# Gated scan layer with a mixture of experts: C's row to its bank by ScalarE, three places for its products, first loads in parts, the norm in pairs, the logits turned inside a product

## Chip, cores and metric

The kernel runs on one core of a Trainium2 chip. The metric is the device time of one execution in microseconds (us). The core's engines are named as in the profile: PE (TensorE), PEld (its weight loads), DVE (VectorE), ACT (ScalarE), POOL (GpSimd) and SP (SyncE, which here only issues DMAs). Each engine runs its own instructions in program order; where this text says that something is queued behind something else, it is this order that is meant.

## What is computed

The input `x` is 4 batches of 512 rows by 512, all float32. Two residual steps are made:

```python
x = x + tanh(g_xattn) * ssm(ctx, z=layernorm(x))      # for each of the 4 batches
x = x + tanh(g_ffn)   * moe(layernorm(x))

# ssm: 512 channels e, 512 times l, 16 states n
u     = silu(conv4(in_proj(ctx)) + b)                 # 512 x 512
dt_lo, B, C = split(x_proj(u))                        # 16, 16 and 16 rows
delta = softplus(dt_proj(dt_lo) + bias)
state[e,n] = state[e,n] * exp(delta[e] * A[e,n]) + delta[e]*u[e]*B[n]   # over l
y[e]  = sum_n state[e,n] * C[n] + D[e]*u[e];  y *= silu(z)

# moe: one shared expert for every row, and for every row the 3 best of 7 experts
p   = softmax(x @ gate_w + gate_b); best 3 of p + biases; weights p / sum of the 3
out = ffn(x, shared) + sum over the 3 of w * ffn(x, expert)
ffn(x, w1, wg, w2) = (silu(x @ w1) * (x @ wg)) @ w2
```

## The kernel before

**Layout.** Channels lie on the partitions, in 4 blocks of 128 (`c`), and times along the free axis. A *step* of a scan loop takes one state `k` and two channel blocks (`W = 2`), so a batch has 32 steps. A step is: POOL multiplies the B row by `delta*u` into `h` (`product`, L581, 128x1024), ACT makes two decays `da = exp(delta*A)` in PSUM (`decay`, L592), DVE runs two scans (L615), and then `finish` (L530 and on) multiplies `h` by the C row and adds the result up.

**Front (L411).** The first batch's projection, convolution, `x_proj` and softplus are made alone. They begin with `in_w` (L93) and the first context `cT` (L103), each one DMA of 512 KB on SP's queue.

**First loop (`loop(0)`, batch 0).** Nothing of the experts runs yet, so TensorE adds up: the products `hc = h*C` are added into four PSUM banks `sums` by an identity (L548). From step 4 on the rule of L525 to L530 holds: every third step's product (`n % 3 == 2`) is made by POOL, which reads the C row from `bc` (the B and C rows, spread over the partitions by DMA, two states to a load of 1 MB), and the other two by DVE, which reads the C row from a PSUM bank, `c_bank`. TensorE writes that bank once for every state:

```python
            if sums is not None and n >= per_load - 1 and c0 + W == NC and k + 1 < NS:
                row = DR + NS + k + 1
                nc.tensor.matmul(
                    c_bank, ident[0:NX, row : row + 1].to_broadcast([NX, P]), ly.xd, start=True, stop=True
                )
```

DVE's `hc` alternate between two places by `n % 2`; POOL's have one of their own. The first loop also carries `ahead_delta`, the projections and half of the softplus of batch 1, one piece to a step (`todo`), and `early`, one piece to every second step: the shared expert's three weights of 1 MB, the clearing of two DRAM tables by `xs<-empty` in 6 DMAs of up to 6 blocks (L177), and the load of batch 1's `x`.

**After a loop (`post(q)`, L677).** For the batch just scanned `y` is turned (L690), added to `x` with statistics (`add_y`, L692), normalised (`row_scale`, L207: a small DVE operation and a power on POOL; `norm`, L698), turned again (`turn_xn`) and copied by ACT (`copy_xn`, L709). All four blocks of 128 rows wait for one `row_scale`.

**Experts (`experts(q)`, L986).** A generator with 54 places to stop, here called pieces 0 to 53. Its head is piece 0 to 12: gate logits `pl` and `lg`, four small turns of the logits `pg` (L762), then the products of the shared expert `p1s` and `p2s` by quarters (`half`, L1005) with silu (`sgs`) and gating (`hidden`) between them, the routing on DVE cut into pieces (`route`, L749), the scatter of rows to `xs` by POOL (L869), and the shared output `pos`. Then 13 tiles of 128 gathered rows follow, three pieces each: a product with `w1`, one with `wg`, one with `w2`, two turns of blocks, and a scatter-add of rows to the output (`add_rows`).

**The order between the two.** The loops of batches 1 to 3 run inside the experts of batches 0 to 2. How many scan steps are issued after which piece is written out by hand in the table `STEPS`: for each `q` one string for `post` and one for `experts`, a digit for each piece. In these loops DVE makes every product with C and every addition (L530, L541). The preparation of batch `b + 2` (`ahead`, L359) is advanced by one piece in pieces 9 to 51 (`prepare`, L1045).

Of the kernel before, what the change touches and what calls it, by code (L numbers as in the profile page):

```python
# [10 lines left out]
F32 = mybir.dt.float32  # L11
# [6 lines left out]
P = 128  # L18
NS = 16
DR = 16  # L20
# [14 lines left out]
    0: ("000000", "010111110011010010101102100111110010011101111101101001"),  # L35
    1: ("100000", "111000110012000200010120111110110110001110111101100101"),
    2: ("001000", "021011010010111100101110200201011100102110010000000000"),
    3: ("000000", "000000000000000000000000000000000000000000000000000000"),
}
# [3 lines left out]
def gated_ssm_moe(  # L43
# [49 lines left out]
    nc.sync.dma_start(in_w, in_wT.rearrange("(k p) e -> p k e", p=P))  # L93
# [4 lines left out]
    def load_ctx(b):  # L98
        if b == 1:
            cT = homes[4][:, 0:NK, :]  # L100
        else:
            cT = one.tile([P, NK, L], F32, tag="cT", name=f"cT_{b}")
        nc.sync.dma_start(cT, ctxT[b].rearrange("(k p) l -> p k l", p=P))  # L103
        return cT
# [68 lines left out]
    def clear():  # L173

        nc.sync.dma_start(acc[(B - 1) * L : (B - 1) * L + P, :], empty[0][:, 0:D])
        for dst, src in zip(xs, empty):
            for i in range(0, NSLOT, 6):  # L177
                k = min(6, NSLOT - i)
                nc.sync.dma_start(
                    dst[i * P : (i + k) * P, :].rearrange("(i p) d -> p i d", p=P),  # L180
                    src.unsqueeze(1).to_broadcast([P, k, D + NW]),
                )
                yield
# [23 lines left out]
    def row_scale(mv, what):  # L207

        n = mv.shape[1]
        ve = small.tile([P, n], F32, tag="ve", name=f"ve_{what}")  # L210
        nc.vector.tensor_scalar(ve, mv[:, :, 1], EPS, None, ALU.add)
        rstd = small.tile([P, n], F32, tag=f"rstd{what[0]}", name=f"rstd_{what}")
        nc.gpsimd.tensor_tensor(rstd, ve, mhalf[:, 0:n], ALU.pow)
        return rstd
# [144 lines left out]
    def ahead(ly):  # L359


        for c in range(NC):
            ly.in_proj(c)
            yield 0.0
            ly.last_tap(c)
            yield 0.0
            ly.other_taps(c)
            later.append(lambda c=c: ly.silu(c))
            yield 2.3

        for _ in range(3):
            if later:
                yield 0.0
        flush()
        ly.x_proj()
        yield 0.0
        ly.rows_out()
        yield 0.0
        for c in range(NC):
            ly.dt_proj(c)  # L380
            yield 0.0
            ly.abs_relu(c)
            if c + 1 < NC:
                yield 0.0
        for c in range(NC):
            ly.exp(c)
        yield 0.0
        for c0 in range(0, NC, 2):
            for c in range(c0, c0 + 2):
                ly.log(c, own=True)  # L390
            yield 0.0
            for c in range(c0, c0 + 2):
                ly.soft(c)
                yield 2.5

    def ahead_delta(ly):
        ly.x_proj()
        yield 0.0
        ly.rows_out()
        ly.dt_proj(0)  # L400
        yield 0.0
        for c in range(NC):
            ly.abs_relu(c)
            if c + 1 < NC:
                ly.dt_proj(c + 1)
                yield 0.0
        for c in range(NC):
            ly.exp(c)
        yield 0.0
# [71 lines left out]
    def loop(b, sums):  # L481
# [29 lines left out]
        def finish(n, h):  # L511
# [3 lines left out]
            cost = 0.0  # L515
            if sums is not None and n >= per_load:
                next(todo, 0.0)
                if n % 2 == 0:
                    next(early, None)
            hc = h if sums is None else held[-1][:, n % 2]  # L520
            late = False
            c_k, engine = ly.bcs[k // NG][:, 1, k % NG, :], nc.vector
            if sums is not None and n >= per_load:

                if n % 3 == 2 and n < last:  # L525
                    engine, late = nc.gpsimd, True
                    hc = one.tile([P, W, L], F32, tag="cT", name=f"hc_{n}")
                else:
                    c_k = c_bank
            engine.tensor_tensor(hc, h, c_k.unsqueeze(1).to_broadcast([P, W, L]), ALU.mult)  # L530
            if sums is not None and n >= per_load - 1 and c0 + W == NC and k + 1 < NS:
                row = DR + NS + k + 1
                nc.tensor.matmul(
                    c_bank, ident[0:NX, row : row + 1].to_broadcast([NX, P]), ly.xd, start=True, stop=True
                )
            if sums is None:
                if nxt is not None and n >= last - W and nxt.n_mul < nxt.n_du:
                    nxt.mul(nxt.n_mul)
                    cost += 0.7
# [18 lines left out]
            return cost  # L558

        def ready(layer, n):  # L560

            k, c0 = steps[n]
            cost = 0.0
            for c in range(c0, c0 + W):
                if k == 0 and layer.n_soft == c:
                    layer.soft(c)
                    cost += 1.4
                if k == 0 and layer.n_mul == c:
                    layer.mul(c)
                    cost += 0.7  # L570
            return cost
# [26 lines left out]
        for n, (k, c0) in enumerate(steps):  # L598
            i = n % per_load
            cost = 3.6 if sums is not None else 4.8  # L600
            if h_before is not None:
                cost += finish(n - 1, h_before)
            if n not in ly.hs:
                cost += ready(ly, n)
                product(ly, n)
            if n not in ly.das:
                decay(ly, n)
            if n < last:
                cost += ready(ly, n + 1)
# [28 lines left out]
            if n >= last - 1 and sums is None:  # L638
                flush()
                gate(n - last + 1)  # L640
                cost += 0.7
            h_before = h
            if n == len(steps) - per_load - 1:

                for d in preps.pop(b + 1, ()):
                    cost += d
            if n == 2 and b > 0 and nxt is not None:
                ctxs[b + 1] = load_ctx(b + 1)
            if b > 0 and k // NG == 5:
                norm_x(b, i)  # L650
                cost += 0.9
            if b > 0 and k // NG == 6 and i == 1:
                szs = silus_x(b)
            yield cost
# [5 lines left out]
        cost = finish(last, h_before)  # L660
# [5 lines left out]
        for d in todo:  # L666
            cost += d
        yield cost + (2.0 if sums is not None else 2.7)
# [8 lines left out]
    def post(q):  # L677
# [20 lines left out]
        def norm(t):  # L698
            nc.vector.tensor_scalar(
                xns[:, t, 0:D], xx[:, t0 + t, :], mv[:, t, 0:1], rstd[:, t : t + 1],  # L700
                ALU.subtract, ALU.mult,
            )
# [14 lines left out]

        each(turn_y, pairs[0])
        yield 1.6, 0.0
        for k, pair in enumerate(pairs):  # L720
            each(add_y, pair)
            if k + 1 < len(pairs):
                each(turn_y, pairs[k + 1])
                yield 1.6, 3.2
        rstd = row_scale(mv, f"f_{q}")
# [5 lines left out]
        yield 0.0, 3.4, True  # L731
        each(norm, pairs[0])
        yield 0.0, 1.4
        for k, pair in enumerate(pairs):
            if k > 0:
                each(copy_xn, pairs[k - 1])
            else:
                for more in pairs[1:]:
                    each(norm, more)
            each(turn_xn, pair)  # L740
            yield 1.8, (1.4 if k == 0 else 0.0)
# [242 lines left out]
    SLOT = 3.75  # L984

    def experts(q):  # L986
# [6 lines left out]
        part = SLOT * nt / NC  # L993
# [11 lines left out]
        def half(k, hc):  # L1005
            pool, tag = (((ps_h, "p1"), (ps_o, "po")), ((ps_h, "p2"), (ps_t, "pt")))[k][hc % 2]
            (p1s, p2s)[k][hc] = mm(
                pool, tag, f"p{k + 1}s_{q}_{hc}", lambda c: ws.t[k][:, c, ts(hc, P)], lambda c: xnT[:, c, :], M
# [11 lines left out]
        yield part, 0.0, True  # L1020
        for hc in range(NC):
            if hc > 0:
                sgs(hc - 1)
            next(way, None)
            if adds:
                adds.pop(0)()
            half(0, hc)
            if hc == 1:
                next(way)
            yield part, (2.8 if hc == 1 else 0.0), hc > 0  # L1030
# [9 lines left out]
            yield part, (0.4, 4.8, 0.7, 0.7)[hc], hc < 2 or None  # L1040
# [3 lines left out]

        def prepare():  # L1045

            return next(preps.get(b + 2, iter(())), 0.0)
# [22 lines left out]
        yield SLOT, prepare(), True  # L1070
        hidden(NC - 1)
        W[1].load(1)
        second(1, range(1, NC - 1))
        second(2, range(2))
        yield SLOT, 0.7 + prepare()
        for i in range(4):
            xt[i] = rows_in(q, i)
        for t in range(2):
            second(t, [NC - 1])
        second(2, range(2, NC))  # L1080
        yield SLOT, prepare()
# [3 lines left out]
        yield SLOT, 0.75 + prepare()  # L1085
# [27 lines left out]
        for i in range(last_tile + 1):  # L1113
# [25 lines left out]
            yield SLOT, 0.7 + prepare()  # L1139
# [12 lines left out]
            yield SLOT + 0.6, prepare()  # L1152
# [25 lines left out]
            yield SLOT + 0.6, prepare(), True  # L1178
# [11 lines left out]
        yield SLOT + 0.6, 0.7, False  # L1190
# [3 lines left out]
        yield SLOT, 0.0  # L1194
# [10 lines left out]
    def moe():  # L1205
# [4 lines left out]
        at = {(q, k): count() for q in range(len(CHUNKS)) for k in range(2)}  # L1210
        for q, (b, _, _) in enumerate(CHUNKS):
# [3 lines left out]
            for _ in posts[q]:  # L1215
                yield q, 0, next(at[q, 0])
            banks = SOME
            for _ in experts(q):
                yield q, 1, next(at[q, 1])
                if q + 1 < len(CHUNKS) and CHUNKS[q + 1][0] in loop_done:  # L1220
                    others, banks = banks, SOME[:2]
                    piece = next(posts[q + 1], None)
                    banks = others
                    if piece is not None:
                        yield q + 1, 0, next(at[q + 1, 0])
# [77 lines left out]
```

## Time and profile before

| | us |
|---|---|
| median of 3 runs | 1098.37 |
| lowest and highest of them | 1097.23 and 1102.14 |
| the profiled execution: its own time | 1101.86 |
| the profiled execution: its span in the profile | 1099.7 |

The profile is of one execution. Its lines give, for groups of instructions, the line of the kernel, the engine, the operation, the tile written and the tiles read, how often, the time busy, the mean time of one in ns, and the idle time before them with what ended it. In the trace a time is counted from the start of the span. The stages, by their main lines: the front until 39 us, the first loop until 168, the first `post` until 194, the experts of batch 0 until about 440, of batch 1 until about 677, of batch 2 until about 894, and those of batch 3, with no loop beside them, until the end.

| engine | busy us | share of the span |
|---|---|---|
| PE | 971.8 | 88% |
| DVE | 795.9 | 72% |
| ACT | 537.7 | 49% |
| POOL | 495.7 | 45% |

### The profile page before, as it was taken

The page shows a single profiled execution, that of the slowest core. Times are in us where ns is not written, and L with a number is a line of the kernel's source. Part 1 is how long each engine was busy: PE and PEld are TensorE (multiplying, and loading weights), DVE is VectorE, ACT ScalarE, POOL GpSimd, SP SyncE. Part 2 cuts the span into 40 slices and gives each one's busy share as a digit, 9 for nine tenths or more (in the row PEclk, how much of TensorE's full clock was granted, in tenths as well). Part 3 has the DMA queues.
Part 4 walks back from the last instruction along what each step waited for, and adds up shares of the span by engine and source line. Part 5 has one row for each costly group of instructions (what it writes and reads, how often), then busy time and mean ns, then how long its engine had stood idle before and what let it go on. Part 6 is the DMA issues. An engine that isn't in the chain of part 4 may idle for free. (4 is left out here: it accounts for less than half of the span.)

```text
span 1099.7 us, 8888 instructions
## 1 busy us (share of the span) xinstructions
PE 971.8 (88%) x2532; PEld 432.4 (39%) x2532; DVE 795.9 (72%) x988; ACT 537.7 (49%) x747; POOL 495.7 (45%) x322
## 2 busy tenths in 40 slices
PE   7479885869999987979999889879999989999995
PEld 2123232324444434434444444334444534444442
DVE  5879887899999999879999998889988321100000
ACT  4566342365588674436597745536574220112211
POOL 1277980392463655572555545754554115011111
PEclk9579788989999999999999999989999999999998
DMA  3136920097999876589899936788999657999974
GB/s 123 58 133 208 362 91 27 10 356 229 336 325 343 292 258 221 143 310 333 303 329 317 355 105 212 258 278 319 308 367 316 194 174 255 344 314 331 322 243 96
DMA packets 137914, 272.10 MB, mean 247 GB/s; under 512 B 17006, under 2 KB 17006, under 8 KB 137854
## 3 DMA queue, kind: packets, MB, share of 16 engines
q1 hardware_dynamic: 126334, 244.71, 64.0%
q0 software_dynamic: 11328, 26.42, 10.4%
q8 instruction: 26, 0.43, 0.1%
q10 hardware_dynamic: 192, 0.26, 0.1%
q14 instruction: 34, 0.28, 0.1%
HBM read 230.65 MB, written 40.71 MB: 247 GB/s over the span
## 5 line engine op out<-in xcount | busy, mean ns | idle before, releaser
L581 POOL TENSOR_TENSOR h<-bc,home 128x1024 f32<-128x1024 f32 x128 | 309.6, 2425 | 248.1 <-DVE home L541 194.2
L917 PE MATMUL p<-w,turned_x 128*128 128x512 f32 x832 | 383.0, 605 | 22.5 <-ACT h L1157 16.5
L615 DVE TENSOR_TENSOR_SCAN h<-da,h 128x512 f32<-128x512 f32 x256 | 297.5, 1207 | 18.6 <-POOL h L581 10.1
L592 ACT ACTIVATE da<-home,a_neg 128x512 f32<-128x512 f32 x256 | 174.2, 689 | 248.1 <-DVE h L615 246.4
L917 PEld LDWEIGHTS p<-w,turned_x 128*128 128x128 f32 x832 | 155.4, 193 | 206.4 <-issue 172.5
L917 PE MATMUL po<-w,turned_h 128*128 128x512 f32 x416 | 189.9, 600 | 10.8 <-ACT yo L951 7.3
L956 POOL DMA_INDIRECT out_dram<-yo,row x52 | 97.3, 1871 | 220.1 <-ACT yo L951 188.4
L1096 DVE TENSOR_TENSOR h<-h,p 128x512 f32<-128x512 f32 x52 | 35.1, 675 | 156.5 <-PE p L917 151.8
L530 DVE TENSOR_TENSOR h<-h,bc 128x1024 f32<-128x1024 f32 x96 | 129.7, 1351 | 1.1
L541 DVE TENSOR_TENSOR home<-home,h 128x1024 f32<-128x1024 f32 x96 | 117.5, 1224 | 3.1
L917 PEld LDWEIGHTS po<-w,turned_h 128*128 128x128 f32 x416 | 75.6, 191 | 90.1 <-issue 76.2
L548 PE MATMUL sum<-hc,ident 128*128 128x512 f32 x128 | 75.3, 737 | 21.2 <-DVE hc L530 20.0
L869 POOL DMA_INDIRECT xs<-xn,place x48 | 55.1, 1147 | 41.9 <-issue 25.1
L1055 PE MATMUL pos<-w_s,home 128*128 128x512 f32 x128 | 60.6, 623 | 10.6 <-DVE home L1016 5.6
L917 PE MATMUL p1s<-home,w_s 128*128 128x512 f32 x128 | 62.0, 629 | 8.5 <-ACT sgs L1013 8.5
L909 ACT COPY turned_x<-pt_x 128x512 f32<-128x512 f32 x52 | 30.2, 580 | 79.0 <-PE pt_x L904 79.0
L592 ACT ACT_TABLE_LOAD x50 | 64.2, 1283 | 0.9
L951 ACT ACTIVATE yo<-po,weight 128x512 f32<-128x512 f32 x52 | 35.4, 681 | 53.6 <-PE po L917 46.1
L917 PE MATMUL p2s<-home,w_s 128*128 128x512 f32 x128 | 57.9, 595 | 0.0
L909 ACT COPY turned_h<-pt_h 128x512 f32<-128x512 f32 x52 | 30.1, 580 | 52.5 <-PE pt_h L904 52.4
L548 PEld LDWEIGHTS sum<-hc,ident 128*128 128x128 f32 x128 | 27.4, 226 | 67.1 <-issue 33.2
L1157 ACT ACT_TABLE_LOAD x36 | 46.2, 1283 | 0.5
(142 smaller groups left out, 828.5 us busy)
## 6 DMA issues: line engine op xcount, KB each, us to landing
w<-in_w_dram SPq DMA_DIRECT2D x104, 1024.0 KB, 8.2
w<-in_wg_dram SPq DMA_DIRECT2D x52, 1024.0 KB, 8.8
bc<-rows SPq DMA_DIRECT2D x32, 1024.0 KB, 5.9
xt<-xs SPq DMA_DIRECT2D x52, 256.0 KB, 5.9
xs<-empty SPq DMA_DIRECT2D x6, 1560.0 KB, 10.3
w_s<-in_ws_dram SPq DMA_DIRECT2D x8, 1024.0 KB, 9.9
xx<-in_x_dram SPq DMA_DIRECT2D x4, 1024.0 KB, 7.6
w_s<-in_wsg_dram SPq DMA_DIRECT2D x4, 1024.0 KB, 11.7
```

The lines of the kernel that those rows point to most:

```text
L530: engine.tensor_tensor(hc, h, c_k.unsqueeze(1).to_broadcast([P, W, L]), ALU.mult)
L541: nc.vector.tensor_tensor(y[:, c0 : c0 + W, :], y[:, c0 : c0 + W, :], h, ALU.add)
L548: nc.tensor.matmul(sums[c1 + w], ident, hc1[:, w, :], start=False, stop=(k1 == NS - 1))
L581: nc.gpsimd.tensor_tensor(h, b_k.unsqueeze(1).to_broadcast([P, W, L]), layer.u[:, c0 : c0 + W, :], ALU.mult)
L592: nc.scalar.activation(da, layer.delta[:, c, :], AF.Exp, scale=a_neg[:, c, k : k + 1])
L615: nc.vector.tensor_tensor_scan(h[:, w, :], da, h[:, w, :], 0.0, ALU.mult, ALU.add)
L869: put = nc.gpsimd.indirect_dma_start(xs[q % 2], bass.IndirectOffsetOnAxis(ap=place[:, t, k : k + 1], axis=0), xns[:, t, :], None)
L909: nc.scalar.copy(t, pt)
L917: nc.tensor.matmul(p[:, 0:n], lhs(c), rhs(c), start=(c == 0), stop=(c == NC - 1))
L956: nc.gpsimd.indirect_dma_start(acc, bass.IndirectOffsetOnAxis(ap=slot_of[q][1][:, i : i + 1], axis=0), yo, None, compute_op=ALU.add,)
L1055: nc.tensor.matmul(pos[t], hTs[:, c, ts(t, P)], ws.t[2][:, c, :], start=(c == 0), stop=(c == NC - 1))
L1157: nc.scalar.activation(hs[i], p1.pop(i), AF.Silu)
```

## The change

Each part in a sentence. (1) `c_bank` is written by a ScalarE copy from `bc` and no more by TensorE. (2) The products with C have three places, by `n % 3`, in all of the first loop. (3) `in_w` comes in two DMAs on SP's queue and the first context in two DMAs on ACT's queue. (4) `early` advances at every step and clears in 12 DMAs of up to 3 blocks. (5) `ahead_delta` has more places to stop, and its four exponentials stand in four pieces. (6) In `post`, `row_scale` is made for each pair of blocks. (7) In the head of the experts the turns of the logits stand in the middle of the first quarter product, after its second block. (8) The load `W[1].load(1)` is issued after the four `rows_in`. (9) The digits of `STEPS` are others. (10) The costs that the generators yielded are gone, and `prepare` is replaced by a table `PIECES` with ones at pieces 9 to 51 for batches 0 and 1, as before.

```diff
 STEPS = {
-    0: ("000000", "010111110011010010101102100111110010011101111101101001"),
-    1: ("100000", "111000110012000200010120111110110110001110111101100101"),
-    2: ("001000", "021011010010111100101110200201011100102110010000000000"),
+    0: ("000000", "011011000210010100110201110111110100110101101201101001"),
+    1: ("100000", "201000110010110110110101210110110110001101201101110001"),
+    2: ("000001", "021011010010102100110110110200200102002011010000000000"),
...
-    nc.sync.dma_start(in_w, in_wT.rearrange("(k p) e -> p k e", p=P))
+    for k in range(NK):
+        nc.sync.dma_start(in_w[:, k, :], in_wT[ts(k, P), :])
...
+        if b == 0:
+            for k in range(NK):
+                nc.scalar.dma_start(cT[:, k, :], ctxT[b, ts(k, P), :])
...
-            for i in range(0, NSLOT, 6):
-                k = min(6, NSLOT - i)
+            for i in range(0, NSLOT, 3):
+                k = min(3, NSLOT - i)
...
     def ahead_delta(ly):
         ly.x_proj()
-        yield 0.0
+        yield
+        yield
         ly.rows_out()
+        yield
         ly.dt_proj(0)
...
         for c in range(NC):
             ly.exp(c)
-        yield 0.0
+            yield
...
             if sums is not None and n >= per_load:
-                next(todo, 0.0)
-                if n % 2 == 0:
-                    next(early, None)
-            hc = h if sums is None else held[-1][:, n % 2]
+                next(todo, None)
+                next(early, None)
+            hc = h if sums is None else (held[-1][:, n % 3] if n % 3 < 2 else one.tile([P, W, L], F32, tag="cT", name=f"hc_{n}"))
...
             if sums is not None and n >= per_load - 1 and c0 + W == NC and k + 1 < NS:
-                row = DR + NS + k + 1
-                nc.tensor.matmul(
-                    c_bank, ident[0:NX, row : row + 1].to_broadcast([NX, P]), ly.xd, start=True, stop=True
-                )
+                nc.scalar.copy(c_bank, ly.bcs[(k + 1) // NG][:, 1, (k + 1) % NG, :])
...
         each(turn_y, pairs[0])
-        yield 1.6, 0.0
-        for k, pair in enumerate(pairs):
-            each(add_y, pair)
-            if k + 1 < len(pairs):
-                each(turn_y, pairs[k + 1])
-                yield 1.6, 3.2
-        rstd = row_scale(mv, f"f_{q}")
+        yield True
+        each(add_y, pairs[0])
+        each(turn_y, pairs[1])
+        yield True
+        scale(0)
+        each(add_y, pairs[1])
...
         each(norm, pairs[0])
+        scale(1)
+        yield True
+        each(turn_xn, pairs[0])
+        each(norm, pairs[1])
+        yield True
+        each(copy_xn, pairs[0])
+        each(turn_xn, pairs[1])
+        yield True
         each(copy_xn, pairs[-1])
...
-            next(way, None)
+            if hc > 0:
+                next(way, None)
             if adds:
                 adds.pop(0)()
-            half(0, hc)
+            half(0, hc, None if hc else lambda: next(way))
...
-        W[1].load(1)
         second(1, range(1, NC - 1))
         second(2, range(2))
...
         for i in range(4):
             xt[i] = rows_in(q, i)
+        W[1].load(1)
```

Here `scale(k)` calls `row_scale` for the two blocks of pair `k`.

## The prediction

> **What bounds the kernel now.** I read the totals first, then the span cut into its stages, then who waits in each stage, then the timeline at the waits that the change touches.
>
> ```profile
> PE 971.8 (88%) x2532; PEld 432.4 (39%) x2532; DVE 795.9 (72%) x988; ACT 537.7 (49%) x747; POOL 495.7 (45%) x322
> ```
>
> No engine is full over the span, so the stages decide. In the table by stage the columns are: stretch, its length, then busy time and count for PE, PEld, DVE, ACT and POOL, granted clock, DMA share, GB/s.
>
> ```profile
> 71.00:168.00 97.00, 85.62 (x154) 29.55 (x154) 85.28 (x76) 47.91 (x72) 78.90 (x34) 0.86 0.67 232
> ...
> 194.00:245.00 51.00, 39.34 (x87) 16.92 (x88) 46.65 (x78) 22.04 (x27) 30.58 (x29) 0.90 0.51 189
> 245.00:402.00 157.00, 148.43 (x403) 66.68 (x402) 147.59 (x158) 107.26 (x147) 77.68 (x36) 0.99 0.91 304
> ```
>
> The first loop (71 to 168) is DVE's: 85.28 of 97.00 busy, so 11.7 us are idle. In the head of batch 0's experts (194 to 245) DVE works 46.65 of 51 us and PE 39.34; PE is the one that waits. In the tiles both are at 94%. After 895 PE runs alone; the chain of waits there is PE products nearly throughout.
>
> Who waits in the first loop (waiter, what ended the wait, total us, times, longest):
>
> ```profile
> DVE hc L530 <- PE c_bank L533: 10.0, 4, 3.3
> ...
> POOL hc L530 <- DVE h L615: 10.3, 5, 3.6
> POOL h L581 <- DMA bc<-rows: 2.6, 2, 2.0
> ...
> ACT da L592 <- DVE h L615: 46.7, 49, 4.6
> ```
>
> One line holds 10.0 of DVE's 11.7 idle us. The timeline shows how it comes about:
>
> ```profile
> 119.78 2.35 POOL L530 TENSOR_TENSOR hc<-h,bc 128x1024 f32<-128x1024 f32 x1
> ...
> 121.80 1.12 PE L533 MATMUL c_bank<-xd,ident 48*128 48x512 f32 x2
> ...
> 122.96 1.22 DVE L530 TENSOR_TENSOR hc<-h,c_bank 128x1024 f32<-128x1024 f32 x1 [2.91 <-PE c_bank L533]
> ```
>
> TensorE's queue is in order. The write of `c_bank` stands behind sums that wait for POOL's product; POOL ends it near 122, and only then the bank is written and DVE goes on. The three other waits are 3.26, 2.58 and 1.26 us; the first (at 82) stands behind batch 1's `dt_proj`.
>
> **1. C's row by ScalarE, three places, exponentials spread (first loop).** Removed: the wait on PE (10.0), one wait on a place of `hc` (0.4) and one on `da` behind four exponentials in a row (0.3): 10.7 us at most. Added: 14 copies of 128x512. Nearest rows: a copy PSUM to SBUF 0.58 us, `da` SBUF to PSUM 0.69, so 8 to 10 us on ACT, which is idle for 49 of the 97. The copy waits for DVE's last product with the old row; queued behind it on ACT are the two `da` of the next step, for which DVE's scans wait. They wait for DVE's scan anyway (the 46.7 above): the copy runs beside a pair of scans of 2.33 us, so it costs nothing; after a step of POOL's it delays a `da` by about 0.25 us, still ahead of its scan. Without that cover it would be 14 x 0.65 = 9 us.
>
> What is late next is POOL. A round of three steps is 6 scans and two products on DVE; undisturbed rounds (106.11 to 115.49, 148.76 to 158.14) take 9.38 us. POOL's round is 4 operations of 2.35 = 9.40. They are level, and DVE's stalls were POOL's slack. POOL's two waits for `bc` (2.6) stay, because that load is issued only after POOL's product has read the buffer, with two operations (4.7 us) to go while it takes 5.2 to 6.6. I take half of the 2.6 as new DVE stalls: gain 10.7 - 1.2 = 9.5. Bounds: 10.7, and 5.5 if both waits double (5.2), for the clearing's DMAs now come in a denser row. In bytes they are the same, before each `bc` at most 3.1 MB, as before; the six further issues (0.5 us each) lie on SP between waits.
>
> One rule speaks against taking work from TensorE here; first the rows:
>
> ```profile
> 39.00:48.00 9.00, 1.32 (x2) 0.00 (x0) 7.23 (x10) 4.62 (x6) 4.65 (x2) 0.50 0.00 0
> ...
> 147.00:157.00 10.00, 6.04 (x13) 1.99 (x12) 9.76 (x10) 4.42 (x8) 8.09 (x4) 0.99 0.22 74
> ```
>
> With PE nearly idle the clock is 0.50; in a stretch of the loop without stalls, with PE 60% busy, it is 0.99. Four sums take 1.98 us at 89.70, at full clock, and 3.78 at 48.75, at half. After the change PE has 12 sums to a round, 12 x 0.43 = 5.2 of 9.38 us, or 56%: nearest to the second row. I charge nothing; the other end is a rival below. The Trainium skill, "TensorE: Matmul & The Clock Gate", Part 1, says that the clock falls to half after an idle window of about 3.4 us. By it the loop would stay warm, since the sums of a round come in three bursts; if all of it ran cold, the gain of this part would be lost, and the sum would show no change.
>
> **2. First loads in parts (front).**
>
> ```profile
> 6.06 9.08 PE L234 MATMUL pin<-cT,in_w 128*128 128x512 f32 x16 [6.06 <-DMA cT<-in_ctxT_dram]
> ```
>
> PE's first product waits for both loads in full. In slices of 1 us the DMAs moved 16, 150, 412, 383, 289 KB from 1 us on: the first 1.05 MB are through at about 5.3, and the product starts 0.75 later. Half of it is through at 3.9, so products of the first halves can start at 4.65; the second halves land by the time that the first block's two instructions (0.85 each) end. Gain 1.4, and ACT and DVE behind it run in a chain, so it carries to the loop. Bounds: 1.9 (SP no longer issues `cT` 0.5 us after `in_w`) and -0.3 (the two issues now stand on ACT ahead of its table load; ACT waits 5.2 us for `gs` anyway).
>
> **3. Norm in pairs.** Before, DVE waited 1.13 us for POOL's power (180.87 to 181.88). After, pair 0 is normalised without that wait, but the second power stands behind it in DVE's order: one more small operation (0.17), then about 1.1 of waiting. DVE ends at about 184.0 and not 183.83; the turns begin 1.1 us earlier and the last copy ends 0.8 earlier. That does not reach the logits: ACT's `lg` at 193.32 was held by `d_u` and `da`, queued before it. I take 0, bounds -0.3 and +0.9. In later batches the pair waits lie under scan steps, or under PE's tiles (848 to 895: PE 44.87 of 47).
>
> **4. Logits turned inside a product.**
>
> ```profile
> 224.19 5.82 PE L917 MATMUL p1s<-home,w_s 128*128 128x512 f32 x8 [6.83 <-ACT sgs L1013]
> ...
> 442.05 0.41 PE L762 MATMUL pg<-ident,lg 7*128 7x7 f32 x4 [0.77 <-ACT lg L758]
> ```
>
> PE waited for `lg` 3.25, 0.77, 0.77 and 0.77 us; half a quarter product (1.7) now covers it. In batch 0 the 1.7 is swallowed by the 6.83 shown. In batches 1 and 2 DVE sets the head; I take 0.4 each. In batch 3 nothing waits later on the chain: 0.77. Routing starts up to 1 us later; under 27 us of products that costs nothing. Sum 1.6, bounds 0.8 and 3.3.
>
> **5. Steps moved, load moved.** The steps per string are the same in total (34, 35, 30), and their running count never differs by more than 2. A step is 2.33 + 1.22 + 1.22 = 4.8 us of DVE. In batch 0's head one step now stands after piece 2 in place of 3, and three move to pieces 9 and 10. The step after piece 2 holds seven softplus operations besides (6 us), now ahead of the routing up to `sel`, so `pc` on PE would wait about 7 us; the old waits (6.8, 2.3, 1.6, 0.9) mostly vanish, and I come to PE 5 us earlier at piece 12, with one step (4.8) left for later, where DVE is 94% busy. Net about 0. `W[1].load(1)` behind `rows_in` is needed some 15 us later: nothing. I take +0.5, bounds -6 and +7, a step and some waits either way.
>
> **Sum.** 1.4 + 9.5 + 0 + 1.6 + 0.5 = 13.0 us. The profiled execution took 1101.86 itself (span 1099.7), so 1088.9 for its like. It lies 3.5 above the median of the runs; against the median 1098.37 it is 1085.4, and I say 1085.
>
> **Rivals.** *POOL takes the bank's place:* DVE's stalls turn into waits for `h`. For it: 9.40 against 9.38 a round, and two `bc` waits without slack. Against it: POOL's starts lie 9.23 apart when it is not held up. Price: 4 us less, 1089.5. *The steps gain too:* PE's idle in 194 to 848 is about 59 us and DVE's 47; a better order takes 10 of them, as with 11.6 us of PE waits in batch 0's head. 1075. *The steps lose:* the new 7 us wait at `pc` is not paid back, with a cold product (5.8 for 3.7) after it: 9 to 10 us, 1095; it makes the whole slower than before from 13, three steps of DVE. *The clock falls in the loop (slower):* PE has 128 instructions there (112 sums, 16 of `x_proj` and `dt_proj`) at 0.43 = 55 us at full clock. At 0.50 that is 110 us, longer than the 97 now; the loop costs 13 more instead of 9.5 less, 1108. It decides below a clock of 55/97 = 0.57; the loop now shows 0.86.
>
> **How the numbers follow.** Forecast (1079 to 1089) 0.56; POOL 0.14; steps gain 0.15; steps lose 0.11; clock 0.04. About 0.5% (5.5 us) is what a measurement of this kernel can tell from no change, so faster means under 1092.9: the forecast, the gain, and most of the POOL case, 0.83; within it 0.10, from the POOL and the losing case; slower 0.07, the clock and the worst of the steps. The range 1074 to 1096 holds the forecast with the bounds of parts 1 and 5, the POOL case, most of the gaining case and half of the losing one.
>
> **What would show it.** Right: no wait of DVE for `c_bank` in the first loop, ACT copies there of about 0.6 us, rounds of 9.4 us, waits of DVE for POOL's `h` of 1 to 2 us in all, the loop 9 us shorter; PE's first product near 4.6; no wait for `lg` in batch 3; a wait for `sel` in batch 0's head. Wrong: waits of DVE for `h` above 5 us in the first loop, a granted clock there near 0.6, or the span from the first `p1s` to the end longer by more than 5 us.

## The result and the profile after

| | before | after |
|---|---|---|
| median, 9 runs of each | 1100.03 | 1090.68 |
| lowest and highest of them | 1096.0 and 1102.95 | 1090.12 and 1094.6 |
| the profiled execution: its own time | 1101.86 | 1090.12 |
| the profiled execution: its span | 1099.7 | 1088.4 |

The ratio of the times is 0.9926, with a 95% interval of 0.9907 to 0.9945: 8.1 us less, 6.1 to 10.2. The forecast was 1085, and 13.0 less for the profiled execution. The two profiled executions are 11.7 apart, but that of before lies 1.8 above its median and that of after is the fastest of its nine; the medians are 9.35 apart. The median of 1090.68 is 1.7 above the forecast's own band (1079 to 1089) and 1.2 above the price of the POOL rival (1089.5).

The totals of the page of after:

```profile
PE 950.8 (87%) x2504; PEld 426.4 (39%) x2504; DVE 793.3 (73%) x992; ACT 541.9 (50%) x759; POOL 492.3 (45%) x326
```

PE has the 28 instructions for `c_bank` less and 21 us less of busy time. Those 14 pairs took about 17 us in the trace of before, from 1.12 us for one to 2.1 where the granted clock was low. By stage (first loop, head of batch 0, tiles; columns as before):

```profile
69.00:160.00 91.00, 68.64 (x128) 25.45 (x128) 85.43 (x76) 54.83 (x86) 78.77 (x34) 0.89 0.69 245
...
186.00:237.00 51.00, 38.43 (x85) 16.90 (x84) 42.71 (x76) 20.17 (x26) 28.61 (x30) 0.87 0.51 188
237.00:394.00 157.00, 151.54 (x411) 68.76 (x409) 151.24 (x162) 108.59 (x149) 78.40 (x35) 0.98 0.90 307
```

The same work of DVE (76 instructions, 85.4 us) takes 91 us in place of 97 in the first loop; the granted clock there is 0.89 and was 0.86. The waits of that loop:

```profile
POOL h L583 <- DMA bc<-rows: 4.9, 3, 2.2
...
DVE hc L541 <- ACT c_bank L543: 2.5, 1, 2.5
...
ACT home L304 <- PE pdt L298: 1.8, 1, 1.8
```

Ten us of waiting for TensorE's bank are gone; one wait of 2.5 us for ScalarE's bank is new, and POOL waits for `bc` three times (4.9 us), where it did twice (2.6).

To see which step of the sum holds, I mark both traces at five points, by starts: DVE's first operation of the convolution, the last gating of `y` in the first loop, the first logits product `pl` of batch 0, that of batch 3, and the end of PE's last product in the chain of waits (PE works on for some 3 us). `after_again` is the same kernel in a later run.

| stretch | before | after | after_again | gain | forecast |
|---|---|---|---|---|---|
| to the convolution | 10.66 | 9.04 | 9.38 | 1.6, 1.3 | 1.4 |
| first loop | 162.31 | 155.37 | 156.83 | 6.9, 5.5 | 9.5 |
| `post(0)` | 13.90 | 12.86 | 13.01 | 1.0, 0.9 | 0 |
| `pl` of batch 0 to `pl` of batch 3 | 707.25 | 704.38 | 705.51 | 2.9, 1.7 | 1.3 |
| to PE's last product | 189.51 | 188.81 | 188.81 | 0.7, 0.7 | 0.8 |
| after that | 16.07 | 17.94 | 18.16 | -1.9, -2.1 | 0 |
| sum | | | | 11.3, 8.0 | 13.0 |

The term that failed is the first loop. The last row comes mostly from one transfer at the end of the chain of waits. After:

```profile
885.25 1.91 PE p1s L923 x4
887.16 0.34 PE pg L768 x4
887.50 1.92 PE p1s L923 x4
...
1071.45 6.15 DMA out_dram<-yo,row
```

And before:

```profile
1084.62 4.72 DMA out_dram<-yo,row
```

The last scatter of rows but one, for which the last one waits, took 6.15 us and 4.72 before. In the other kernels' profiles that last stretch is 16.9 to 18.2 us, also where the code of before stands there; the 16.07 of before is the shortest of all, so this row tells more of one execution than of the change. The first three lines show part 4 in batch 3: the turns `pg` stand between the halves of `p1s`, with no wait.

### The profile page after: what moved, and what is told of

The parts are those of the page before. It is cut to its first block, busy times and chain, and to the rows that moved or that the text cites. A ratio compares the mean times of both kernels' runs of the same rounds, so it can differ in the third digit from the quotient of the medians.

```text
span 1088.4 us, 8877 instructions
## 1 busy us (share of the span) xinstructions
PE 950.8 (87%) x2504; PEld 426.4 (39%) x2504; DVE 793.3 (73%) x992; ACT 541.9 (50%) x759; POOL 492.3 (45%) x326
## 5 line engine op out<-in xcount | busy, mean ns | idle before, releaser
L923 PE MATMUL p<-w,turned_x 128*128 128x512 f32 x832 | 377.3, 597 | 14.0 <-ACT h L1158 10.4
L962 POOL DMA_INDIRECT out_dram<-yo,row x52 | 94.3, 1813 | 213.7 <-ACT yo L957 188.7
L541 DVE TENSOR_TENSOR h<-h,bc 128x1024 f32<-128x1024 f32 x96 | 125.7, 1310 | 1.0
L555 PE MATMUL sum<-hc,ident 128*128 128x512 f32 x128 | 72.7, 719 | 39.8 <-DVE hc L541 22.1
L1056 PE MATMUL pos<-w_s,home 128*128 128x512 f32 x128 | 62.9, 645 | 10.4 <-DVE home L1020 9.0
L923 PE MATMUL p1s<-home,w_s 128*128 128x512 f32 x128 | 59.1, 600 | 1.7 <-ACT sgs L1017 1.7
## 6 DMA issues: line engine op xcount, KB each, us to landing
w_s<-in_ws_dram SPq DMA_DIRECT2D x8, 1024.0 KB, 10.2
```

Source lines behind the costliest of these rows:

```text
L555: nc.tensor.matmul(sums[c1 + w], ident, hc1[:, w, :], start=False, stop=(k1 == NS - 1))
L923: nc.tensor.matmul(p[:, 0:n], lhs(c), rhs(c), start=(c == 0), stop=(c == NC - 1))
L962: nc.gpsimd.indirect_dma_start(acc, bass.IndirectOffsetOnAxis(ap=slot_of[q][1][:, i : i + 1], axis=0), yo, None, compute_op=ALU.add,)
L1056: nc.tensor.matmul(pos[t], hTs[:, c, ts(t, P)], ws.t[2][:, c, :], start=(c == 0), stop=(c == NC - 1))
```

## What held the first loop: theories

The timeline of after at the one wait that is left:

```profile
86.45 1.12 PE L298 MATMUL pdt<-xd,dt_w 16*128 16x512 f32 x2 [1.66 <-ACT z L312]
88.93 1.12 PE L298 MATMUL pdt<-xd,dt_w 16*128 16x512 f32 x2 [1.35 <-ACT z L312]
89.98 5.40 PE L555 MATMUL sum<-hc,ident 128*128 128x512 f32 x8
91.53 4.65 POOL L583 TENSOR_TENSOR h<-bc,home 128x1024 f32<-128x1024 f32 x2 [2.21 <-DMA bc<-rows]
95.31 1.12 PE L298 MATMUL pdt<-xd,dt_w 16*128 16x512 f32 x2
96.47 0.69 ACT L304 ACTIVATE home<-pdt,pr 128x512 f32<-128x512 f32 x1 [1.84 <-PE pdt L298]
98.14 0.60 ACT L543 COPY c_bank<-bc 128x512 f32<-128x512 f32 x1
98.77 1.22 DVE L541 TENSOR_TENSOR hc<-h,c_bank 128x1024 f32<-128x1024 f32 x1 [2.52 <-ACT c_bank L543]
```

Read from the end: DVE waits for the copy; the copy stands on ACT behind the softplus of batch 1's fourth block (L304), which waits for its `pdt`, the product of `dt_proj`; that product stands on PE behind eight sums that ran at part of the clock (5.40 us; eight at full clock take 3.6 to 3.7), after PE had waited twice for ACT to empty the one PSUM bank that `pdt` goes round through. POOL's wait for `bc` lies in the same time.

*The first theory* was that this place of the copy in ACT's order costs the missing 3 us. *Its rival* was POOL: it is at par with DVE, and the denser DMAs of `early` delay its `bc`. *A second question* is how much the copy brings without the places and the pieces beside it, and a *third* whether the end follows the loop. Times below are medians, ratios are to the kernel before on the same chip with the 95% interval, and waits are of the profiled execution.

## Experiments on the first loop

**copy_ahead.** The copy is issued ahead of the step's piece of batch 1.

```diff
-                next(todo, None)
                 next(early, None)
...
                 nc.scalar.copy(c_bank, ly.bcs[(k + 1) // NG][:, 1, (k + 1) % NG, :])
+            if sums is not None and n >= per_load:
+                next(todo, None)
```

> The changed kernel with one edit: in the first loop the copy of C's row to its bank is issued ahead of the batch-1 piece of that step (its relu, abs and exponential) and not behind it. Theory ACT queue: the one wait left on the bank (2.5 us at 98.8) is the copy standing behind a relu that waits for TensorE; the wait goes, and the loop's last gate comes at about 161.9 instead of 164.4, the whole at about 1088.2. Rival POOL at par: POOL waited 2.2 us for the B and C rows at 91.5 and has no slack left, so DVE's 2.5 us only turn into waits for POOL's h; the last gate moves by 0.7 us or less, the whole stays at 1090.7 within 1.

Measured: 1094.04, ratio 0.9935 [0.9915, 0.9955]; first loop 159.21. No wait for the bank is left, and the loop is 2 to 4 us longer. The lateness came out elsewhere: DVE waits 2.2 us for a decay that now stands behind the softplus, and 1.9 us for PE's sums; ACT waits 4.9 us for `pdt`, behind eight sums of 6.20 us. So the place of the copy alone isn't the cause; what is late is the piece. The theory of the copy's place, by which the whole was to be near 1088, is refuted.

**early_slow.** `early` again at every second step, six blocks to a clearing, as before.

```diff
-            for i in range(0, NSLOT, 3):
-                k = min(3, NSLOT - i)
+            for i in range(0, NSLOT, 6):
+                k = min(6, NSLOT - i)
...
-                next(early, None)
+                if n % 2 == 0:
+                    next(early, None)
```

> The changed kernel with the early loads as before: one piece at every second step, the clearing in 6 DMAs of up to 6 blocks. POOL's wait for the rows at 91.5 (2.2 us) should go, because one load of 1 MB less and no clearing lies ahead of that load. Theory POOL at par: the loop's last gate comes 1.5 to 2.2 us earlier, near 162.5. Theory ACT queue: the wait on the bank behind the relu stays and hides it; last gate within 0.7 of 164.4. The whole: 1088.7 or 1090.7.

Measured: 1091.6, ratio 0.9897 [0.9871, 0.9922]; first loop 159.36 in its profile, which has the longest time of its six runs. The third `bc` wait is gone, as the rival has it, but the bank wait is longer. The waits of its first loop:

```profile
DVE hc L542 <- ACT c_bank L544: 4.3, 1, 4.3
...
ACT home L304 <- PE pdt L298: 3.5, 1, 3.5
...
POOL h L584 <- DMA bc<-rows: 2.8, 2, 2.1
```

POOL is held less, and DVE waits for the same late copy longer. In the loop of this one profile neither theory holds alone. By the ratio the kernel is none the worse for it: 0.9897 beside the 0.9926 and 0.9918 of after, with intervals that overlap.

**copy_ahead_early_slow.** Both edits.

> Both edits together: the copy ahead of batch 1's piece, and the early loads as before. If the two waits (ACT's queue, POOL's rows) cover each other, either alone gives less than 1 us and both give 2.5 to 3: last gate near 161.7, the whole near 1088. If only the ACT queue counts, this is equal to the first alone; if only POOL counts, equal to the second alone.

Measured: 1093.59, ratio 0.9922 [0.9899, 0.9945]; first loop 159.28. Two edits against two causes, and nothing gained: the late `pdt` is still there, whoever waits for it.

**pieces_apart.** So the piece itself: one more stop between the softplus's first part and the next `dt_proj`, which gives `pdt` a step of its own for its way round.

```diff
             ly.abs_relu(c)
             if c + 1 < NC:
+                yield
                 ly.dt_proj(c + 1)
```

> The changed kernel with one more place to stop in batch 1's projections in the first loop: dt_proj of the next block is issued one step after relu and abs of the last, not in the same step, so that TensorE never waits for ACT to free the one spare bank nor ACT for TensorE within a step. Theory round trip: this exchange (PE waits 1.7 and 1.4 us, then sums at half clock, then ACT waits 1.8 us with the bank's copy behind it) makes the 2.5 us that are left; they go, the last gate comes at 161.5 to 162.5, the whole near 1088. Rival POOL at par: last gate at 164, with waits of DVE for h in their place. Rival clock: the clock falls all the same in the loop's thinner stretch, and the waits only change their place: last gate 164 to 168.

Measured: 1093.12, ratio 0.9911 [0.988, 0.9943], with `after_again` beside it at 1094.43, 0.9918 [0.9893, 0.9943]. ACT's wait for `pdt` falls to 0.2 us and DVE's for the bank is gone, so the cause of that wait is found; the first loop takes 155.97, no less than the 155.37 and 156.83 of after. What DVE waits for now in the middle of the loop:

```profile
DVE h L617 <- POOL h L584: 1.7, 3, 0.9
...
ACT home L304 <- PE pdt L298: 0.2, 1, 0.2
```

POOL is the next limit, 1.7 us of it, with 4.5 us of waits for `bc`; at the last gatings DVE waits another 2.8 us for PE's sums, where it waited 2.5 in before.

TensorE's clock has a part in the late piece that no run takes away. In the kernel after and its variants with this wait, the eight sums ahead of `pdt` took 5.09 to 6.33 us. ACT waited 1.8 to 2.8 us where they took 5.4 or less (`after`, `after_again`, `old_steps`), and 3.5 to 4.0 where they took 5.9 or more (the three experiments above). In `pieces_apart` the sums are as slow (twelve in 8.45 us, at full clock 5.42), but ACT hardly waits for what stands behind them.

**apart_slow_scale.** `pieces_apart` and `early_slow` together, and the second power of `post` issued ahead of the first pair's `norm`.

```diff
+                yield
...
-                next(early, None)
+                if n % 2 == 0:
+                    next(early, None)
...
+        scale(1)
         each(norm, pairs[0])
-        scale(1)
```

> A version made from what the runs show: the changed kernel with batch 1's dt_proj and relu in steps of their own, the early loads as before (no 2.2 us of POOL waiting for the rows at 91.5), and the second pair's scale made ahead of the first pair's norm in post. Theory POOL at par: with both hindrances gone the loop is 1.5 to 2 us shorter than the changed kernel's (154 from tap to gate), and post 0.8 shorter; the whole 2 us under the changed kernel. Rival clock: TensorE's clock falls in other stretches, the waits come back at the gates or for h, and the whole is the changed kernel's within 1 us.

Measured: 1089.05, ratio 0.9872 [0.9846, 0.9897], against 1102.73 for before on that chip: the best of all versions run. The first loop takes 154.01, the shortest. Its waits in 65 to 165:

```profile
DVE home L524 <- PE sum L557: 3.3, 4, 1.2
...
POOL h L585 <- DMA bc<-rows: 2.8, 2, 2.1
...
DVE h L618 <- POOL h L585: 2.3, 1, 2.3
```

The 3.3 us are the last gatings. The 2.3 us of DVE are the loop's first step, as in after; no wait for the bank is left, and no wait for POOL later on. The loops (155.4 and 156.8 with neither edit, 156.0 with the pieces, 159.4 with the DMAs, 154.0 with both) would fit two causes side by side, of which one shows when the other is gone, but they are one profile each, and two of the same kernel lie 1.5 apart. The ratios (0.9926 and 0.9918; 0.9911; 0.9897; 0.9872) go down at each step, with overlapping intervals but for the last against after's 0.9926. All five runs of this version (1086.33 to 1089.88) lie below all fifteen of after (1090.12 to 1099.05), so the edits together gain, as far as runs at different times can say; how much each does by itself stays open. The moved `scale(1)` did nothing: `post(0)` takes 12.94, as in after.

**bank_by_pe.** The kernel after with TensorE writing the bank again.

```diff
-                nc.scalar.copy(c_bank, ly.bcs[(k + 1) // NG][:, 1, (k + 1) % NG, :])
+                row = DR + NS + k + 1
+                nc.tensor.matmul(
+                    c_bank, ident[0:NX, row : row + 1].to_broadcast([NX, P]), ly.xd, start=True, stop=True
+                )
```

> The changed kernel with C's row written to its bank by TensorE again, all else as changed. Forecast's theory: 8 to 10 us of waits for the bank return in the first loop, last gate near 172, the whole near 1098. Rival, places and pieces: the third place and the spaced pieces had already taken much of it, the waits return with 4 us or less, last gate near 168, the whole 1092 to 1095.

Measured: 1097.73, ratio 0.993 [0.9904, 0.9957]; first loop 165.12. The waits:

```profile
DVE hc L541 <- PE c_bank L544: 12.0, 5, 4.5
```

With everything else of the change in place, the copy is worth 8.3 to 9.8 us of the first loop in the profiles, and 12.0 us of waiting appear without it. By medians 3.3 us of that reach the end (1097.73 against 1094.43), by the ratios 0.4 to 1.3 us (0.993 against 0.9926 and 0.9918), and the intervals overlap. The profiled executions are 6.2 apart, but this one is the second slowest of its six and that of `after_again` the second fastest. So the copy's gain in the loop is shown in the profiles, and its gain in the whole is not shown.

**before_copy_only**, **before_copy_places**, **before_copy_pieces**, **before_copy_both.** From the other side: the kernel before with the copy alone, then with the three places, with the new pieces, and with both.

```diff
-                row = DR + NS + k + 1
-                nc.tensor.matmul(
...
+                nc.scalar.copy(c_bank, ly.bcs[(k + 1) // NG][:, 1, (k + 1) % NG, :])
```

> The kernel before with one edit alone: C's row copied to its bank by ScalarE in place of TensorE's product. Theory of the forecast: the 10.0 us of DVE waiting for the bank go, nearly all; the last gate of the first loop moves from 173.0 to about 164.5 to 166, the whole is 6 to 8 us shorter, about 1093. Rival: in the kernel before the four exponentials of batch 1 stand in one piece and the projection in a shorter row of pieces, so ACT's queue holds the copy back more than in the changed kernel (two waits of 2 to 3 us), and the edit alone brings 4 us or less. Rival POOL: waits of DVE for h of 3 us and more.

> The kernel before with ScalarE's copy and the three places for products with C. First loop counted from the first convolution tap to the last gate: 162.3 us in the kernel before, 159.5 with the copy alone (1.4 us of waits for the bank, 2.6 for TensorE's sums before a product, 3.3 at the gates), 155.4 and 156.8 in two profiles of the changed kernel. Theory places: DVE's waits for sums (2.6) go with the third place, and the loop is 156.5 to 157. Rival pieces: TensorE is late because batch 1's projection exchanges with ACT in its old row; the loop stays at 159 and the wait moves to the bank's copy.

> The kernel before with ScalarE's copy and the longer row of batch 1's pieces, two places as before. Theory pieces: the loop is 156.5 to 157. Theory places: it stays at 159 to 160, with 2 to 3 us of DVE waiting for sums.

> The kernel before with the copy, the three places and the longer row of pieces; the early loads, the front, the norm, the logits and the steps as before. If these three make the changed kernel's first loop, tap to gate is 155.5 to 157, 5 to 7 us less than before, whatever the early loads do. The whole is 1095 to 1098: the front's 1.4 us, the norm's 1 and the logits' and steps' share are missing. Rival: the old digits of the steps lose it again in the experts, as with the copy alone, and the whole is above 1100.

| | median | ratio | first loop |
|---|---|---|---|
| before (profile) | | | 162.31 |
| copy only | 1105.38 | 1.0025 [1.0006, 1.0044] | 159.45 |
| copy, places | 1106.34 | 1.0041 [1.0021, 1.0061] | 156.85 |
| copy, pieces | 1106.62 | 1.0032 [1.0014, 1.005] | 163.05 |
| copy, both | 1101.91 | 0.9994 [0.9972, 1.0015] | 154.83 |

In the loop the copy alone brings 2.9 us, with the places 5.5, with places and pieces 7.5; with the pieces but without the third place the loop is no shorter than before (163.05). The waits of the kernel with copy and pieces, but two places by `n % 2`, show what the third place is for:

```profile
DVE hc L532 <- ACT c_bank L534: 5.3, 1, 5.3
...
DVE hc L532 <- PE sum L547: 2.9, 2, 2.5
```

DVE's product waits for a place that PE's sums still read. So the ten us were not for the copy to give back by itself: the third place takes away a wait that would otherwise take the bank's place. The pieces add 2.0 us to that, hardly more than the 1.5 between two profiles of one kernel. None of these four is faster than before, though, whatever its loop gained: three are slower, by 0.25 to 0.41%, and the fourth is the same. The forecasts for the whole, 1093 for the copy alone and 1095 to 1098 for both, are missed; the rival of the old digits had the last one above 1100.

## Experiment on the steps

**old_steps.** The kernel after with the digits of before.

```diff
-    0: ("000000", "011011000210010100110201110111110100110101101201101001"),
+    0: ("000000", "010111110011010010101102100111110010011101111101101001"),
...
```

> The changed kernel with the digits of the table of steps as before, all else as changed. Forecast: the moved steps bring 0.5 us, bounds -6 and +7; so the whole is at 1091 within 3, PE's wait for the routing's sel (7.6 us) in batch 0's head goes, and the waits for sgs (6.8, 2.3) come back there. Rival: the order was made for the new lengths, and the old digits lose 5 to 8 us in the experts, as the kernel before with the copy alone did (it lost 7 us after its first loop): the whole 1096 to 1099. The first loop is the same in both.

Measured: 1095.84, ratio 0.9936 [0.9911, 0.9961]; in its profile `pl` of batch 0 to `pl` of batch 3 takes 708.33, against 704.38 and 705.51 with the new digits. By medians the digits bring 1.4 us (1095.84 against 1094.43), which the intervals can't tell from nothing; in the profiles 2.8 to 4.0. There the eight profiles with the new digits all show 703.2 to 705.5, and the six with the old ones 707.1 to 714.0.

The third question stays half open. From the end of the first loop to PE's last product before takes 910.66 in its profile; the four kernels above, with the same digits, take 917.34, 914.88, 915.12 and 912.12, `old_steps`, with the new `post` and turns besides, 909.84, and after 906.05. So in the profiles the kernels with the copy take longer behind the loop under the digits of before, also the one whose loop is no shorter (915.12): an earlier end of the loop is not what decides it. One place where two kernels differ is the first product of batch 1's experts. In the kernel with the copy alone the timeline has:

```profile
431.52 3.65 PE L704 MATMUL pn<-ident,xn 128*128 128x128 f32 x16 [3.10 <-PEq L962]
436.09 5.91 PE L753 MATMUL pl<-home,gw 128*7 128x512 f32 x8 [0.92 <-ACT home L707]
```

And in after:

```profile
426.42 3.60 PE L762 MATMUL pl<-home,gw 128*7 128x512 f32 x8 [2.17 <-ACT home L709]
```

In `after_again`, which is the same kernel:

```profile
427.37 5.55 PE L762 MATMUL pl<-home,gw 128*7 128x512 f32 x8 [1.64 <-ACT home L709]
```

The same eight instructions take 5.91 us, 3.60 and 5.55, at about 0.6 of the clock and at full clock, after idle times of about 3 us nearby. Such a product costs 1.7 to 2.3 us more. But it falls on either side in two executions of one kernel, and before, with the old digits, has 3.60 there too. So this shows how some microseconds come and go, not that the old digits lose them here; where they lose stays open. In the kernel with copy, places and pieces, PE's busy time between these points is even 4.4 us less than before (832.99 against 837.40) and its idle time 5.9 more, so the clock isn't all of it. And its profiled execution, at 1096.91, was the fastest of twelve with a median of 1101.91: the 6.0 us by which PE ended earlier in that profile are not what the kernel does in the median.

## Why the prediction was right or wrong

**The old wait** was read wrongly in one point. The prediction has the bank's write at 121.80 stand behind sums that wait for POOL's product. That product ended at 122.13, when the write had begun. Between the writes the trace of before has:

```profile
113.70 8.16 PE L548 MATMUL sum<-hc,ident 128*128 128x512 f32 x12
```

and by stretch, for the slow ones among them:

```profile
113.70:119.00 5.30, 5.30 (x8) 2.20 (x8) 5.20 (x6) 2.27 (x5) 5.30 (x3) 0.50 1.00 297
```

PE had no idle time there, and the granted clock was 0.50. Twelve such sums took 5.42 us at 94.06, so 2.7 of the 2.91 us that DVE waited are this difference (an estimate). The waits near 144 and 164 stand behind such sums too: the granted clock was 0.50 from 133.5 to 139 and 0.52 from 156.7 to 160. It was a late queue of PE's, then, and not POOL that DVE waited for; a bank that PE doesn't write is the way out of either. But "I charge nothing" for the clock left out what makes that queue late, in before as in after.

**Part 1, the loop, is the term that was mis-sized:** 9.5 forecast, 6.9 and 5.5 measured, near the lower bound given. The gain was to come from taking the wait on PE away, and in the loop it did. The step that failed is "the copy runs beside a pair of scans of 2.33 us, so it costs nothing". It named what is queued behind the copy on ACT and not what the copy is queued behind: a softplus piece that waits for `pdt`, hence for PE's sums at part of the clock, the very queue that the bank was taken out of. The step "I take half of the 2.6 as new DVE stalls" failed in the same direction: the prediction counted bytes ahead of each `bc` and found them unchanged, at most 3.1 MB, but POOL's waits grew to 4.9, as three weight loads of 1 MB, the clearing of the output and a part of the tables' clearing, some 4 MB, came to stand ahead of one `bc` load. Taking away both brings the loop to 154.01, 8.3 less than before.

**The rival "POOL takes the bank's place"** is half true: 9.40 against 9.38 a round made POOL the next limit as soon as the late copy was gone (`pieces_apart`), for less than 2 us.

**Part 2** is right, to the place:

```profile
4.41 9.03 PE L246 MATMUL pin<-cT,in_w 128*128 128x512 f32 x16 [4.41 <-DMA cT<-in_ctxT_dram]
```

PE starts at 4.41, forecast 4.65 (in the other profiles with these loads at 4.25 to 5.05), and DVE 1.6 and 1.3 earlier, forecast 1.4.

**Part 3** was taken at 0 and brings 1.0. Its timeline:

```profile
169.09 0.70 POOL L225 TENSOR_TENSOR rstd_f<-ve_f,mhalf 128x2 f32<-128x2 f32 x1 [12.36 <-DVE ve_f L223]
...
173.97 1.00 DVE L698 TENSOR_SCALAR xn<-xx,mv_f,rstd_f 128x512 f32<-128x512 f32 x2 [0.82 <-POOL rstd_f L225]
```

The power for two columns takes 0.70 us, and for four it took 1.0, so DVE's second wait is 0.8 and not 1.1. And the step "that does not reach the logits" was wrong: all of the stretch up to `pl` came forward, with what stands ahead of `lg` on ACT. From the last gating to `lg` it is 20.3 to 20.4 us in the five profiles with the old norm and 19.1 to 19.5 in the nine with the new one.

**Parts 4 and 5** came out as worked in the head of batch 0 and in batch 3. The head in the timeline:

```profile
184.44 0.42 PE L768 MATMUL pg<-ident,lg 7*128 7x7 f32 x4 [0.85 <-ACT lg L764]
...
201.23 0.60 PE L811 MATMUL pc<-sel,before 128*128 128x28 f32 x2 [7.60 <-DVE sel L808]
...
235.09 9.73 PE L1056 MATMUL pos<-w_s,home 128*128 128x512 f32 x16 [4.96 <-DVE home L1020]
```

The wait for `sel` was forecast at about 7 us and is 7.60; from the last gating to the first gathered rows' turns `post` and head take 81.36 before, 80.25 and 79.35 after, and 80.14 with the old digits. About 1.0 of what is gained is that of `post`, so the moved steps come to little in that head, as said. Over all three batches they bring 2.8 to 4.0 by the profile of `old_steps`, within the bounds of -6 and +7, where 0.5 was taken. Batch 3 gains 0.7 where 0.77 was forecast. The rest of batches 0 to 2 gains 0.4 to 1.6 more than the 1.3 taken.

**The clock rival**, a loop at half clock throughout, did not come: the loop shows 0.89. **That the steps lose** did not come either. What the sum left out is that microseconds gained in the loop need not arrive: it carried part 1's gain to the end in full, while `bank_by_pe` shows 3.3 of 8 to 10 us arriving by medians, and `before_copy_both` almost none of its 7.5. The loops are of one execution each, so it isn't shown whether the rest gives the gain back or the other executions' loops gain less.

By the times of the whole, then, the 8.1 us can't be put down to part 1. Without the copy the ratio is 0.993, with the old digits 0.9936, both within the interval of after, and the copy, the places and the pieces alone have 0.9994. The profiles give the loop 6.9 of 11.3 us, in one execution of each. If part 1 brings less, the front, the norm, the turns, the early loads and the digits must bring more than the forecast had for them. No run takes the front, the norm or the turns away, so this stays open, and that the total came within the stated range may be luck in part.

## What to carry to other kernels

When a piece of work is moved to another engine's queue, look at what it is queued behind as well as at what is queued behind it, and follow that back one engine further: here the way led back to the queue that the work had left. Where several resources are nearly level (DVE 9.38, POOL 9.40 a round, one spare PSUM bank, loads just in time), expect each wait that is taken away to show the next one: the copy alone gained 2.9 us of the loop where the whole of part 1 gained 6.9 and 5.5, and the whole kernel was then no faster. And judge a shorter stage by the median of the whole: here two kernels had a loop 2.9 and 5.5 us shorter in their profiles (`before_copy_only`, `before_copy_places`) and were slower in all. Whether the fixed order of the steps, written by hand for the old timing, gave the gain back is not shown.

## What the runs showed of the hardware

The fastest and the slowest execution of one kernel can differ in the mean granted clock of TensorE: of the twelve of `before_copy_both` the fastest had 0.956 and the slowest 0.940, for 1096.91 and 1108.42 us; of after, 0.948 and 0.940, for 1090.12 and 1094.6. With `before_copy_only` it is only 0.948 and 0.946, for 1100.52 and 1107.96, so the mean clock doesn't tell all. Differences of a few us between two profiles are therefore no proof of a change.

The Trainium skill, "TensorE: Matmul & The Clock Gate", Part 1, puts the fall to half clock behind an idle window of about 3.4 us. Here waits below that were followed by slow products, and the same wait by both: behind 2.17 us the eight instructions of batch 1's `pl` took 3.60 us in after and 5.30 in `before_copy_both`, with 3.01 and 2.83 us of idle time ahead of the turns before it. In the first loop of before the granted clock was 0.50 from 113.7 to 119, and PE's longest idle time between 71 and there was 1.98 us. So in a schedule with gaps of 2 to 3 us the clock isn't to be had from the length of one gap.
